# 64 rows for the last layer's pair products and the attention cells' state products, two blocks side by side in the array's row halves

## The chip, the cores and the metric

The kernel runs on one core of one Trainium2 chip. The time is device microseconds of one execution; the median of three runs is given. A profile is one further execution, recorded by the hardware profiler. The engines are called TensorE (PE, its weight loads PEld), VectorE (DVE), ScalarE (ACT), GpSimd (POOL) and SyncE (SP).

## What is computed

Four graph layers over 4096 nodes with 64 features follow each other, each as x = layernorm(x + layer(x, adj)). adj is a dense 4096 x 4096 matrix in f32.

- Layer 0 is a Chebyshev sum: three successive products with adj.
- Layer 1 has two gated cells, one over the products of the masks adj > 0 and adj < 0 with x, and one over an attention whose scores depend only on the sign of an edge. The cell's part that the change touches is the state product:

```python
gi = x @ w_ih.T + b_ih
gh = h @ w_hh.T + b_hh          # the state product
r = sigmoid(ir + hr); z = sigmoid(iz + hz); n = tanh(inn + r * hn)
return (1.0 - z) * n + z * h
```

- Layer 2 is a sum over neighbours with weights that decay with the neighbour's rank.
- Layer 3 is hyperbolic. For each pair (i, j) it needs the Moebius difference of x_i and x_j, its norm, an arctanh, and a sum over j weighted by adj. The kernel gets all pairs from one quantity per pair, a matrix product of prepared left and right sides (a "pair product"), and a second small product, here called the opposite term, that marks pairs on different sides of the unit ball.

## The kernel before

The nodes are 32 blocks of 128; four blocks are a group (8 groups), and adj is read in tiles of 512 x 512. The stages follow each other in one program for each engine. TensorE, VectorE, ScalarE and GpSimd each run their instructions in the order of the program; the order is set when the program is built, from the order of the source, and `in_order` (`tc.keep_in_program_order`) holds the marked instructions of an engine to the source's order among themselves. Waits between engines are semaphores.

1. **First pass** (to 363 us): adj is loaded, turned by TensorE (L604), copied by ScalarE (L611) and stored turned. The weights for later layers are loaded and turned meanwhile, one step a tile (`attention_weights`, `state` at L399 to L406).
2. **Second and third pass** (to 566 us). Third-pass rows end with `normed_third` (layer norm, `centre` at L298 to L302) and, some tiles later, `turned_third`, which turns the group's rows into columns of `tr_a` with `to_columns`: four transposes (L213) and one copy (L214). Row 64 of `tr_a` holds ones, for the biases. For the last row this is done by a step inside the attention stage.
3. **Attention** (to 852 us): for each group, 8 tiles of masks (VectorE L448; stored by GpSimd at L741) are multiplied with x (L1004, L1012) and adj with x (L1021). After a group, its cells are worked off one step a tile (`group_end`). `gates` (L797 to L807) does, block by block, the state product (L801: 128 rows of `tr_a`, of which 65 are used, times 260 or 256 columns) and for the edge cell the input products (L805) into the same PSUM bank. Two blocks share a PSUM tile; for the last group, whose cells run inside the decay stage, one block at a time.
4. **Decay** (to 1062 us): counts (L1242, into two column halves) give weights (L1247), which multiply x (L1198, L1210) in the array's two row halves. Groups are done in two turns of four. At a turn's end `ends` normalises the groups, `prepare` makes their left sides (`lx`, 66 columns: x, and two more) and the marks of their side of the ball (`sides`, 2 columns), and `turn_prepared` turns both with `to_columns`, eight transposes and two VectorE copies a group. The first four groups' ends fall in the second turn, the last four groups' in the pairs stage.
5. **Pairs** (from 1062 us): 36 tiles (i, j) in 72 half tiles, here called units; 64 are whole (two blocks of 128 by 512 columns), 8 on the diagonal are half as wide. For each unit `product` (L1359) multiplies two blocks of left sides with a right side (`right`, L1315 to L1319), `square` (L1368, ScalarE) and `opposite` (L1377) follow, then ScalarE Ln and Exp (L1550, L1551), VectorE L1575, ScalarE L1577 and L1586, VectorE L1560 and L1563; `turn` (L1403) transposes the factors for the mirrored tile and VectorE multiplies them in (L1405); `gather` (L1419, L1424) sums both tiles into two column halves of one bank, and VectorE adds the mirrored sums up (L1435). `less_one` is L1385. PSUM has two buffers for `product` and two for the transposes (`post`). Remaining steps (`seam`) are put in one a unit: ends of the last four groups, and each finished group's `finals`.

An f32 matmul is two instructions on TensorE, a transpose one.

Of the kernel before, what the change touches and what calls it, by code (L numbers as in the profile page):

```python
# [27 lines left out]
V_FLOOR = 2.0**-21  # L28
# [32 lines left out]
def gnn4_kernel(  # L61
# [107 lines left out]

    sp_two = keep.tile([P, NB, 2 * F], BF16, name="sp_two")  # L170
# [45 lines left out]
    def to_rows(pool, src, w):  # L216

        ps = pool.tile([P, GB, w], F32, name="post", tag="post")
        for b in range(GB):
            nc.tensor.transpose(ps[:, b, :], src[:, cols(b)], ident[0:w, 0:w])  # L220
        return ps

# [120 lines left out]
    def attention_weights(wp, wps):  # L343
# [6 lines left out]
        rows = {name: wp.tile([F + 1, H3], F32, name=f"row_{name}") for name in ("hhe", "hhn")}  # L350
        acol = wp.tile([F, 2], F32, name="acol")
# [7 lines left out]
        def load_biases(dst, name, b_ih, b_hh):  # L359
            nc.gpsimd.memset(dst, 0.0)  # L360
            nc.scalar.dma_start(dst[F : F + 1, F:GC], b_ih.unsqueeze(0))
            nc.scalar.dma_start(rows[name][F : F + 1, :], b_hh.unsqueeze(0))

        def load_rest():
# [8 lines left out]
            lambda: load_biases(whh_e, "hhe", b_ih_e, b_hh_e),  # L373
            lambda: load_biases(whh_n, "hhn", b_ih_n, b_hh_n),
# [24 lines left out]
        def state(name, dst):  # L399
            ps = turned(name)  # L400
# [5 lines left out]
            nc.vector.tensor_scalar_mul(dst[:, 0:F], dst[:, 0:F], 0.5)  # L406

# [12 lines left out]
        def score_weights():  # L420
# [17 lines left out]
            lambda: state("hhe", whh_e), lambda: state("hhn", whh_n), turned_gat, gat_and_cell, score_weights,  # L438
# [37 lines left out]
    with tc.tile_pool(name="acc", bufs=1) as acc_p, tc.tile_pool(  # L476
# [207 lines left out]
        def turned_third(g):  # L684
            to_columns(ps_p, tr_a[0 : F + 1, gcols(g)], nat_a[:, gblocks(g), :], F + 1, nc.scalar.copy)
# [47 lines left out]
    tr_o = sp_two.rearrange("p b f -> p (b f)")  # L733
# [41 lines left out]
    def group_end(g, Q, nb, tl, sums, a_t, wq, by_ln=False):  # L775
# [20 lines left out]
        def gates(ps_p, h, whh, w, pairs):  # L796
            for bs in blocks(h):  # L797
                got[bs.start] = ps = new(ps_p)
                for i in range(nb):
                    b = bs.start + i  # L800
                    in_order(nc.tensor.matmul(  # L801
                        ps[:, i, 0:w], lhsT=tr_a[:, cols(g * GB + b)], rhs=whh, start=True, stop=(not pairs)
                    ))
                    for m, (t, wt) in enumerate(pairs):
# [163 lines left out]
    def attention(signed, cols_p, sg, tl, ps_a, ps_p):  # L968
# [60 lines left out]
        else:  # L1029
# [7 lines left out]
        steps = [nothing, nothing, nothing, lambda ps_p: to_columns(  # L1037
            ps_p, tr_a[0 : F + 1, gcols(last_row)], nat_a[:, gblocks(last_row), :], F + 1, nc.scalar.copy
        )]
# [49 lines left out]
    nc.gpsimd.memset(tr_o, 0.0)  # L1089
# [3 lines left out]
    sides = const.tile([P, NB, 2], F32, name="sides")  # L1093
# [4 lines left out]
    def prepare(g):  # L1098
# [3 lines left out]
        sq = sm.tile([P, GB, F], F32, name="sq", tag="t0")  # L1102
        nc.vector.tensor_tensor(sq, xg, xg, ALU.mult)
        nc.vector.tensor_reduce(n2[:, gs], sq, AX.X, ALU.add)
        nc.vector.tensor_scalar(inside[:, gs], n2[:, gs], -1.0, 1.0, ALU.mult, ALU.add)
        nc.vector.tensor_scalar(sides[:, gs, 0], inside[:, gs], 0.0, None, ALU.is_ge)
        nc.vector.tensor_scalar(sides[:, gs, 1], inside[:, gs], 0.0, None, ALU.is_lt)
        nc.vector.tensor_tensor(side[:, gs], sides[:, gs, 0], sides[:, gs, 1], ALU.subtract)
# [3 lines left out]
        lx = sm.tile([P, GB, F + 2], F32, name="lx")  # L1112
        nc.vector.tensor_tensor(lx[:, :, F + 1], rabs[:, gs], side[:, gs], ALU.mult)
        nc.vector.tensor_tensor(lx[:, :, F], n2[:, gs], lx[:, :, F + 1], ALU.mult)
        nc.vector.tensor_tensor(lx[:, :, 0:F], xg, over_rows(lx[:, :, F + 1]), ALU.mult)
        nc.vector.tensor_tensor(nat_c[:, gs, 0 : F - 1], nat_a[:, gs, 0 : F - 1], over_rows(rabs[:, gs], F - 1), ALU.mult)
        nc.vector.scalar_tensor_tensor(nat_c[:, gs, F - 1], n2[:, gs], 1.0, rabs[:, gs], ALU.add, ALU.mult)
        left[g] = lx

    def turn_prepared(ps_p, g):  # L1120
        to_columns(ps_p, tr_a[0 : F + 2, gcols(g)], left.pop(g), F + 2, nc.vector.tensor_copy)
        to_columns(ps_p, tr_o[0:2, gcols(g)], sides[:, gblocks(g), :], 2, nc.vector.tensor_copy)

    def constants3():


        to_right = const.tile([P, F + 2], F32, name="to_right", tag="wih_pp")
        to_other = const.tile([P, 2], BF16, name="to_other", tag="wih_mm")

        spread = const.tile([P, F + 1], F32, name="spread", tag="whh_e")  # L1130
        wh_x = const.tile([P, F], F32, name="wh_x", tag="whh_n")
        nc.vector.memset(to_right, 0.0)
        nc.vector.tensor_scalar_mul(to_right[0:F, 0:F], ident[0:F, 0:F], -4.0)
        nc.vector.tensor_scalar_mul(to_right[F : F + 2, F : F + 1], ident[F : F + 2, F + 1 : F + 2], 2.0)
        nc.vector.tensor_scalar_mul(to_right[F : F + 2, F + 1 : F + 2], ident[F : F + 2, F : F + 1], 2.0)
        nc.vector.memset(to_other, 0.0)
        nc.vector.tensor_scalar_mul(to_other[0:2, 0:1], ident[0:2, 1:2], OPPOSITE)
        nc.vector.tensor_scalar_mul(to_other[0:2, 1:2], ident[0:2, 0:1], OPPOSITE)
        nc.vector.memset(wh_x, 0.0)
        nc.vector.tensor_copy(wh_x[0:F, :], wh)  # L1140
# [152 lines left out]

    with tc.tile_pool(name="o3", bufs=1) as op, tc.tile_pool(name="cols3", bufs=3) as cols_p, tc.tile_pool(
# [14 lines left out]
        for t in rvs + ros:  # L1309
            nc.gpsimd.memset(t, 0.0)  # L1310

        def right(i):
            q = seq.index(i) % 2
            ps = ps_p.tile([P, GW], F32, name="post", tag="post")
            nc.tensor.matmul(ps[0 : F + 2, :], lhsT=to_right, rhs=tr_a[:, gcols(i)], start=True, stop=True)  # L1315
            nc.scalar.copy(rvs[q][0 : F + 2, :], ps[0 : F + 2, :])
            ps = ps_p.tile([P, GW], F32, name="post", tag="post")
# [322 lines left out]
```

## Time and profile before

| | us |
|---|---|
| median of three runs | 1538.62 (1536.35 to 1538.94) |
| the profiled execution's own time | 1536.75 |
| its span, first to last instruction | 1535.0 |
| TensorE, VectorE, ScalarE, GpSimd busy in the span | 1408.3, 1064.4, 762.8, 124.4 |
| mean granted TensorE clock | 0.979 |

An engine's busy time is the union of its instructions. TensorE's instructions are pipelined and their ends are modelled, so its rate is read from the distance between starts. A row of a group reads: line, engine, operation, output <- inputs, partitions x elements and type, for a matmul the rows*columns of the array in front of it, then count, busy time, mean length, idle time before and what ended it. "Idle, by X" names the instruction whose semaphore came last. The chain of work that ended last is, by engine, 65% TensorE, 20% VectorE, 7% ScalarE and 5% DMA.

### The profile page before, as it was taken

The numbers are of one execution on the slowest core, as the hardware profiler recorded it, in microseconds if no ns is written. First come the engines' busy times: TensorE is split into PE (matmuls) and PEld (weight loads), VectorE is DVE, ScalarE is ACT, GpSimd is POOL, SyncE is SP. The second block draws the span as 40 slices with busy tenths as digits, with TensorE's granted clock in tenths as the row PEclk, the third lists the DMA queues.
The fourth block names the chain that finished last, engine by engine and source line by source line (L and its number), as shares of the span: only waits on it lengthen the run. The fifth ranks groups of instructions, "written<-read, shape, count | busy, mean of one in ns | idle before, by whom it ended". The sixth has DMA issues, their size and how long they took to land.

```text
span 1535.0 us, 19444 instructions
## 1 busy us (share of the span) xinstructions
PE 1408.3 (92%) x7054; PEld 645.1 (42%) x7054; DVE 1064.4 (69%) x2121; ACT 762.8 (50%) x1267; POOL 124.4 (8%) x194
## 2 busy tenths in 40 slices
PE   5999999999999999889999999998888999899995
PEld 3555555554444333334443333333334434344343
DVE  5889989883000675657677322645999999899997
ACT  3554444432000111212222576655877999899995
POOL 3001100000000011222222200000000000000000
PEclk9999999999999999999999999999999999999997
DMA  9999999996787998878887655453134443445330
GB/s 291 411 406 409 413 409 399 385 357 265 247 278 270 373 387 322 278 280 316 301 317 286 193 170 176 155 165 156 65 141 155 170 168 138 167 160 191 150 114 11
DMA packets 103361, 385.40 MB, mean 251 GB/s; under 512 B 16340, under 2 KB 17368, under 8 KB 71256
## 3 DMA queue, kind: packets, MB, share of 16 engines
q1 hardware_dynamic: 84256, 296.78, 54.1%
q0 software_dynamic: 15616, 85.73, 13.7%
q10 hardware_dynamic: 3384, 1.56, 0.4%
q8 instruction: 58, 0.95, 0.2%
q14 instruction: 47, 0.39, 0.1%
HBM read 297.26 MB, written 85.20 MB: 249 GB/s over the span
## 4 chain that ended last, share of the span: by engine, by line
PE 65%; DVE 20%; ACT 7%; DMA 5%; issue 3%; SPq 0%; ACTq 0%; POOL 0%; DVEq 0%; POOLq 0%
PE tp L604 7%; PE pass L512 6%; PE w_ps L512 6%; PE v_ps L1359 5%; PE sums_ps L1419 4%; PE a_ps L1021 4%; PE cnt_ps L1242 4%; PE acc_ps L1198 4%; PE pass L505 4%; PE h_ps L505 4%; DVE at_m L1405 3%; DVE rt L1575 3%; PE p_ps L1004 2%; PE post L523 2%; ACT wt L1247 2%
## 5 line engine op out<-in xcount | busy, mean ns | idle before, releaser
L611 ACT COPY at<-tp 128x512 f32<-128x512 f32 x256 | 132.5, 599 | 134.6 <-issue 93.7
L1359 PE MATMUL v_ps<-rv,tr_a 128*128 128x512 f32 (+1 forms) x288 | 138.4, 604 | 33.6 <-DVE rt L1575 29.9
L1247 ACT ACTIVATE wt<-cnt_ps 128x512 uint16<-128x512 f32 x210 | 116.4, 594 | 73.8 <-PE cnt_ps L1242 69.6
L604 PE MATMUL tp<-ident,raw 128*128 128x128 f32 x1024 | 133.2, 284 | 14.5 <-DMA raw<-in_adj_dram 9.7
L637 DVE TENSOR_REDUCE dpart<-raw 128x4 f32<-128x2048 f32 x64 | 145.4, 2272 | 0.1
L639 DVE TENSOR_REDUCE lows<-raw 128x1 f32<-128x2048 f32 x64 | 145.4, 2272 | 0.0
L1419 PE MATMUL sums_ps<-at_d,nat_c 128*64 128x512 f32 x288 | 143.2, 619 | 1.4 <-DVE at_d L1563 1.0
L604 PEld LDWEIGHTS tp<-ident,raw 128*128 128x128 f32 x1024 | 116.5, 145 | 53.5 <-issue 30.7
L1021 PE MATMUL a_ps<-at,nat_a 128*64 128x512 f32 x512 | 126.3, 622 | 2.9 <-DVE at L987 2.9
L448 DVE TENSOR_SCALAR pos<-at 128x2048 fp8e4<-128x2048 f32 x72 | 87.6, 1232 | 49.3 <-DMA at<-adj_t 43.3
L1424 PE MATMUL sums_ps<-at_m,nat_c 128*64 128x512 f32 x224 | 111.0, 618 | 0.0
L512 PE MATMUL w_ps<-at,cheb_n 128*128 128x512 f32 x224 | 101.1, 595 | 0.0
L512 PE MATMUL pass<-at,cheb_n 128*128 128x512 f32 x224 | 98.3, 596 | 0.7 <-DVE cheb_n L665 0.7
L1586 ACT ACTIVATE rt<-rt,one_col 128x1024 f32<-128x1024 f32 x72 | 78.7, 1095 | 21.6 <-DVE rt L1575 21.4
L1359 PEld LDWEIGHTS v_ps<-rv,tr_a 128*128 128x128 f32 x288 | 51.9, 195 | 82.8 <-issue 43.4
L1242 PE MATMUL cnt_ps<-m,follow 128*64 128x512 fp8e4 x480 | 81.2, 391 | 5.1 <-ACT wt L1247 2.0
L1575 DVE SCALAR_TENSOR_TENSOR rt<-v_ps,rt 128x1024 f32<-128x1024 f32 x72 | 83.4, 1159 | 3.1 <-ACT rt L1551 2.9
L1560 DVE SCALAR_TENSOR_TENSOR f<-rt,w 128x1024 f32<-128x1024 f32 x72 | 83.0, 1160 | 1.3 <-ACT rt L1586 1.3
L1563 DVE TENSOR_TENSOR at_d<-at_d,f 128x1024 f32<-128x1024 f32 x72 | 83.4, 1159 | 0.1
L1405 DVE TENSOR_TENSOR at_m<-post,at_m 128x512 f32<-128x512 f32 x112 | 75.3, 685 | 10.1 <-PE post L1403 9.5
L1368 ACT ACTIVATE w<-v_ps,one_col 128x1024 f32<-128x1024 f32 x72 | 75.7, 1053 | 11.5 <-PE v_ps L1359 11.0
L1577 ACT ACTIVATE w<-w,half_shift 128x1024 f32<-128x1024 f32 x72 | 78.6, 1094 | 0.8
(368 smaller groups left out, 2269.7 us busy)
## 6 DMA issues: line engine op xcount, KB each, us to landing
at<-adj_t SPq DMA_DIRECT2D x122, 1024.0 KB, 6.6
raw<-in_adj_dram SPq DMA_DIRECT2D x64, 1024.0 KB, 12.3
adj_t<-at POOLq DMA_DIRECT2D x64, 1024.0 KB, 8.1
at_d<-adj_t SPq DMA_DIRECT2D x36, 1024.0 KB, 4.8
at_m<-adj_t SPq DMA_DIRECT2D x28, 1024.0 KB, 6.8
mask_t<-pos POOLq DMA_DIRECT2D x64, 256.0 KB, 6.2
m<-mask_t SPq DMA_DIRECT2D x120, 128.0 KB, 2.8
m<-mask_t SPq DMA_DIRECT2D x60, 256.0 KB, 4.0
```

Source lines behind the costliest of these rows:

```text
L505: in_order(nc.tensor.matmul(ps[q * F : (q + 1) * F, :], lhsT=cheb_n[:, jb, k, :], rhs=rhs, start=first, stop=last, skip_group_check=True,))
L512: in_order(nc.tensor.matmul(ps, lhsT=cheb_n[:, jb, k : k + 2, :], rhs=rhs, start=first, stop=last))
L604: in_order(nc.tensor.transpose(tp[:, cols(b)], raw[:, b, cols(k)], ident))
L611: nc.scalar.copy(at[:, k, :], tp)
L637: in_order(nc.vector.tensor_reduce(dpart[:, g, c, :], raw, AX.X, ALU.add))
L639: in_order(nc.vector.tensor_reduce(lows[:, n : n + 1], raw.rearrange("p b j -> p (b j)"), AX.X, ALU.min))
L1021: in_order(nc.tensor.matmul(ps[q * F : (q + 1) * F, :], lhsT=nat_a[:, c * CB + k, 0:F], rhs=parts[q if signed else 0][:, k, :], start=(c = ...
L1242: in_order(nc.tensor.matmul(cnt[a][r * HP : (r + 1) * HP, :], lhsT=follow, rhs=chunks[c][odd][2 * a + r][:, k, :], start=(h == 2 * NB - 1) ...
L1247: in_order(nc.scalar.activation(wt[odd][a], cnt[a], AF.Relu, scale=-128.0))
L1359: nc.tensor.matmul(vs[n][:, k, cs], lhsT=tr_a[:, cols(jb)], rhs=rights[i][0][:, cs], start=True, stop=True)
L1419: in_order(nc.tensor.matmul(bank[0:F, :], lhsT=nat_c[:, j * CB + k, :], rhs=own[t][:, k, :], start=(i == j and k == 0), stop=(j == seq[-1] ...
L1575: nc.vector.scalar_tensor_tensor(rt, vs[n][:, :, cs], V_FLOOR, rt, ALU.max, ALU.add)
```

## The change

The left sides, the marks and the state are brought to 64 rows (features), and two neighbouring blocks are stacked: block 2m in rows 0 to 63, block 2m + 1 in rows 64 to 127. A pair product or a state product then uses 64 rows, and two neighbouring blocks use the two row halves. To make 64 rows enough, x being centred (its features sum to nothing), the 64th feature is left out: its place holds ones in the state, whose weights have the 64th column subtracted (`leave_out`) and the bias in its row, and a second quantity in the left sides. The constant 1 that was added by the bias of Square and Ln goes into the product itself.

Rows are turned by `turn_pairs` (third pass, state) and the new `turn_prepared`: two 128 x 128 transposes instead of four.

```diff
+    tr_x = tr_a[:, 0 : N // 2].rearrange("p (m n) -> p m n", n=P)
...
+    def turn_pairs(pool, g):
+        t = sm.tile([P, GB, F], F32, name="with_ones", tag="t0")
+        nc.gpsimd.memset(t[:, :, F - 1], 1.0)
+        nc.scalar.copy(t[:, :, 0 : F - 1], nat_a[:, gblocks(g), 0 : F - 1])
+        ps = pool.tile([P, GB // 2, P], F32, name="post", tag="post")
+        for m in range(GB // 2):
+            nc.tensor.transpose(ps[:, m, :], t[:, 2 * m : 2 * m + 2, :].rearrange("p b f -> p (b f)"), ident)
+        nc.scalar.copy(tr_x[:, g * GB // 2 : (g + 1) * GB // 2, :], ps)
...
+        def both_halves():
+            nc.gpsimd.memset(twice, 0.0)
+            for q in range(2):
+                nc.vector.tensor_copy(twice[0:F, q * F : (q + 1) * F], ident[0:F, 0:F])
+                nc.vector.memset(twice[F : F + 1, (q + 1) * F - 1 : (q + 1) * F], 1.0)
...
-        def state(name, dst):
-            ps = turned(name)
+        def state(name, to):
+            for t in range(2):
+                leave_out(raws[name][:, t, :])
+            ps, dst = turned(name), states[name]
...
+            w = to.shape[1]
+            ps = wps.tile([P, w], F32, name=f"state_ps_{name}", tag="post")
+            nc.tensor.matmul(ps, lhsT=twice, rhs=dst[:, 0:w], start=True, stop=True)
+            nc.scalar.copy(to, ps)
...
         def turned_third(g):
-            to_columns(ps_p, tr_a[0 : F + 1, gcols(g)], nat_a[:, gblocks(g), :], F + 1, nc.scalar.copy)
+            turn_pairs(ps_p, g)
...
+    tr_c = tr_x
+    tr_o = sp_two[:, 0 : NB // 2, :]
...
                 for i in range(nb):
                     b = bs.start + i
+                    half = slice(b % 2 * F, b % 2 * F + F)
                     in_order(nc.tensor.matmul(
-                        ps[:, i, 0:w], lhsT=tr_a[:, cols(g * GB + b)], rhs=whh, start=True, stop=(not pairs)
+                        ps[:, i, 0:w], lhsT=tr_x[half, (g * GB + b) // 2, :], rhs=whh[half, :],
+                        start=True, stop=(not pairs)
                     ))
+                for i in range(nb):
+                    b = bs.start + i
                     for m, (t, wt) in enumerate(pairs):
...
-        steps = [nothing, nothing, nothing, lambda ps_p: to_columns(
-            ps_p, tr_a[0 : F + 1, gcols(last_row)], nat_a[:, gblocks(last_row), :], F + 1, nc.scalar.copy
-        )]
+        steps = [nothing, nothing, nothing, lambda ps_p: turn_pairs(ps_p, last_row)]
...
-    nc.gpsimd.memset(tr_o, 0.0)
...
+        sides = sm.tile([P, GB, F], F32, name="sides", tag="o_sb")
+        nc.gpsimd.memset(sides, 0.0)
...
-        lx = sm.tile([P, GB, F + 2], F32, name="lx")
-        nc.vector.tensor_tensor(lx[:, :, F + 1], rabs[:, gs], side[:, gs], ALU.mult)
-        nc.vector.tensor_tensor(lx[:, :, F], n2[:, gs], lx[:, :, F + 1], ALU.mult)
-        nc.vector.tensor_tensor(lx[:, :, 0:F], xg, over_rows(lx[:, :, F + 1]), ALU.mult)
...
+        lx = sm.tile([P, GB, F], F32, name="lx")
+        nc.vector.tensor_tensor(lx, nat_c[:, gs, :], over_rows(side[:, gs]), ALU.mult)
+        left[g] = lx, sides
...
-        to_columns(ps_p, tr_a[0 : F + 2, gcols(g)], left.pop(g), F + 2, nc.vector.tensor_copy)
-        to_columns(ps_p, tr_o[0:2, gcols(g)], sides[:, gblocks(g), :], 2, nc.vector.tensor_copy)
+        ps = ps_p.tile([P, 2 * GB // 2, P], F32, name="post", tag="post")
+        ms = slice(g * GB // 2, (g + 1) * GB // 2)
+        for n, t in enumerate(left.pop(g)):
+            for m in range(GB // 2):
+                two = t[:, 2 * m : 2 * m + 2, :].rearrange("p b f -> p (b f)")
+                nc.tensor.transpose(ps[:, n * GB // 2 + m, :], two, ident)
+        nc.vector.tensor_copy(tr_c[:, ms, :], ps[:, 0 : GB // 2, :])
+        nc.vector.tensor_copy(tr_o[:, ms, :], ps[:, GB // 2 : GB, :])
...
-        for t in rvs + ros:
-            nc.gpsimd.memset(t, 0.0)
         def right(i):
...
+            for to, w, t in ((rvs[q], to_right, tr_c), (ros[q], to_other, tr_o)):
+                ps = ps_p.tile([P, GW], F32, name="post", tag="post")
+                for b in range(GB):
+                    nc.tensor.matmul(
+                        ps[:, cols(b)], lhsT=w[:, b % 2, :], rhs=t[:, (i * GB + b) // 2, :], start=True, stop=True
+                    )
+                nc.scalar.copy(to, ps)
...
-                nc.tensor.matmul(
-                    vs[n][:, k, cs], lhsT=tr_a[:, cols(jb)], rhs=rights[i][0][:, cs], start=True, stop=True
-                )
+                half = slice(jb % 2 * F, jb % 2 * F + F)
+                in_order(nc.tensor.matmul(
+                    vs[n][:, k, cs], lhsT=tr_c[half, jb // 2, :], rhs=rights[i][0][half, cs], start=True, stop=True
+                ))
...
-            nc.scalar.activation(ws[n][:, :, cs], vs[n][:, :, cs], AF.Square, bias=one_col)
+            nc.scalar.activation(ws[n][:, :, cs], vs[n][:, :, cs], AF.Square)
...
-                nc.tensor.matmul(
-                    vs[n][:, k, cs], lhsT=tr_o[:, cols(jb)], rhs=rights[i][1][:, cs], start=False, stop=True,
-                    skip_group_check=True,
-                )
+                half = slice(jb % 2 * F, jb % 2 * F + F)
+                in_order(nc.tensor.matmul(
+                    vs[n][:, k, cs], lhsT=tr_o[half, jb // 2, :], rhs=rights[i][1][half, cs],
+                    start=False, stop=True, skip_group_check=True,
+                ))
...
+            for q in range(2):
+                half = slice(q * F, (q + 1) * F)
+                nc.vector.tensor_copy(wh_x[half, q, :], spread_w[half, :])
...
-                nc.vector.scalar_tensor_tensor(rt, vs[n][:, :, cs], V_FLOOR, rt, ALU.max, ALU.add)
+                nc.vector.scalar_tensor_tensor(rt, vs[n][:, :, cs], 1.0 + V_FLOOR, rt, ALU.max, ALU.add)
...
-                nc.scalar.activation(rt, rt, AF.Ln, bias=one_col)
+                nc.scalar.activation(rt, rt, AF.Ln)
```

The constants of the last layer (`constants3`, made at the start of the decay layer's second turn) are laid out for both halves: `to_right` and `to_other` become 128 x 2 x 128, `wh_x` 128 x 2 x 64, and 22 small VectorE operations make them instead of 12. The steps of `finals` read the stacked columns with `wh_x` of the block's half, in as many matmuls as before.

## The prediction

> **What bounds the kernel now.** I read the page's 40 slices first, then the busy time by stage, then who waits for whom inside the two stages that the change touches, then the instructions of single steps. TensorE is busy for 92% of the span, but that is a mean over five stages: a first pass over the adjacency (to 363 us), two more passes (to 566), the attention layer (to 852), the decay layer (to 1062) and the last layer's pairs (to the end).
>
> By stage (columns: length, then busy time of TensorE, its weight loads, VectorE, ScalarE, GpSimd, granted clock, DMA share, GB/s):
> ```profile
> 0.00:363.00 363.00, 339.51 (x1789) 201.46 (x1790) 306.45 (x269) 155.76 (x307) 46.67 (x90) 0.99 1.01 386
> ...
> 566.00:852.00 286.00, 263.94 (x1261) 111.34 (x1260) 185.80 (x537) 59.71 (x123) 71.49 (x95) 0.97 0.82 296
> 852.00:1062.00 210.00, 201.65 (x1658) 72.73 (x1657) 82.51 (x287) 126.04 (x239) 6.23 (x10) 0.99 0.51 155
> 1062.00:1535.00 473.00, 409.63 (x1692) 183.07 (x1691) 436.08 (x827) 404.73 (x566) 0.00 (x0) 0.96 0.38 143
> ```
> The first pass is the DMA's (share 1.01). Attention and decay are TensorE's. In the pairs stage VectorE is the busiest: 436 of 473 us, TensorE 410, ScalarE 405. So a gain on TensorE there counts only where VectorE waits for it. Those waits, 1062 to 1510 us:
> ```profile
> DVE at_m L1405 <- PE post L1403: 9.5, 10, 2.2
> DVE w L1385 <- ACT w L1368: 4.8, 2, 4.0
> DVE tb L1435 <- PE sums_ps L1424: 3.6, 4, 2.4
> DVE rt L1575 <- ACT rt L1551: 2.9, 4, 1.5
> DVE tr_a L214 <- PE post L213: 1.3, 1, 1.3
> ```
> VectorE is idle for 27 of these 448 us; 15 are put down to TensorE, 10 to ScalarE. The 15 are the heart of the forecast.
>
> One pair unit on TensorE (start, length, line):
> ```profile
> 1305.49 1.98 PE L1359 MATMUL v_ps<-rv,tr_a 128*128 128x512 f32 x4 [0.36 <-DVE rt L1575]
> 1307.41 0.64 PE L1419 MATMUL sums_ps<-at_d,nat_c 128*64 128x512 f32 x1
> 1307.41 0.64 PE L1424 MATMUL sums_ps<-at_m,nat_c 128*64 128x512 f32 x1
> ...
> 1308.75 0.59 PE L1424 MATMUL sums_ps<-at_m,nat_c 128*64 128x512 f32 x1
> 1309.28 0.60 PE L1377 MATMUL v_ps<-ro,sp_two 128*128 128x512 bf16 x2
> 1309.72 0.60 PE L1403 MATMUL post<-ident,f 128*128 128x128 f32 x4
> ```
> Starts count, not lengths (ends are modelled). An f32 matmul is two instructions, 0.43 us apart. The product (two blocks, four instructions) takes 1.92 us to the next start. The sums of L1419 and L1424 go to two column halves and start together: two for the time of one. After the last of them, 1308.75 + 0.43 = 1309.18, the next form starts 0.10 us late: the price of a change of form. The opposite term takes 0.44, eight transposes 8 x 0.109 = 0.87. Unit: 1.92 + 1.87 + 0.44 + 0.87 = 5.1 us. VectorE's starts are 1.13 apart (three long operations) and 0.60 (three short): 5.2 us. ScalarE has five of about 1.0: 5.1. All three engines are level, which is why small delays become idle time.
>
> Row halves, as the change uses them, occur in the decay layer, in bf16:
> ```profile
> 959.66 0.39 PE L1198 MATMUL acc_ps<-wt,over_two 64*128 64x512 bf16 x1
> 959.66 0.39 PE L1198 MATMUL acc_ps<-wt,sup_two 64*128 64x512 bf16 x1
> 959.88 0.38 PE L1198 MATMUL acc_ps<-wt,over_two 64*128 64x512 bf16 x1
> ```
> Two start together, the next pair 0.22 later: full overlap. f32 in row halves is not in this trace. Its bounds: no overlap (1.72 us for four instructions) to full (0.86). I take full, because bf16 row halves and f32 column halves both show it.
>
> **The change, part by part.**
>
> *Pair products and opposite term.* Product 1.72 to 0.86, opposite 0.43 to 0.22: minus 1.08 us per unit. Forms now change four times per unit instead of twice: plus 0.2. TensorE's unit falls from 5.1 to 4.2. Over 64 whole and 8 half units that is some 73 - 15 us less TensorE; making the right sides in eight instructions of 128 columns and four bf16 ones instead of two and one adds 0.2 to 0.8 (at 0.11 to 0.19 each, start spacing or weight load) eight times, say 4. None of that is on the path by itself. What is: of the 15 us VectorE waits for TensorE I take 13 away. What is late next is VectorE itself, then ScalarE.
>
> *No bias in Square and the last Ln.* L1550 (Ln, no bias) is 1049 ns, L1586 (Ln, bias tile) 1142, same shapes. So 0.09 twice a unit off ScalarE, 12 us in all; on the path 2 of the 10 us that VectorE waits for it.
>
> *Preparing the sides.* Per group VectorE loses copies of 682 and 668 ns and two operations of 160, and gains two copies of 128x256 (423 for such a read of PSUM): minus 0.8. Four groups are prepared in the pairs stage, where VectorE sets the pace: minus 3.3, plus 0.4 for two 64x64 copies (180). Four transposes instead of eight save TensorE 0.44 a group; four groups fall in the decay layer, which is TensorE's: minus 1.7. There the constants take ten more small VectorE operations (about 0.15), covered by an engine busy 82 of 210 us; uncovered they cost 1.5. The last group's cells work block by block, so their eight state products overlap with nothing and only change form: plus 1. Decay layer: minus 0.5. GpSimd's dropped fills are covered already.
>
> *State products in the cells.* Around one group's edge gates:
> ```profile
> 785.96 0.71 PE L801 MATMUL post<-whh_e,tr_a 128*128 128x260 f32 x2
> 786.50 0.49 PE L805 MATMUL post<-wih_pp,p_t 128*128 128x196 f32 x2
> 786.83 0.60 PE L801 MATMUL post<-whh_e,tr_a 128*128 128x260 f32 x2
> ```
> A block's state product is two instructions, 0.22 apart. Edge: four blocks, 1.74 us, halved saves 0.87, three more changes of form cost 0.30 to 0.45. Node: 0.87 saved; one of its two pairs stands between 128x128 forms (L895, L1004), 0.2 to 0.3 more; the other already stands between L1021s. Together minus 1.1 a group. From 705 us the period is 34.6 us, TensorE busy 32.7, DMA share 0.83 to 0.91: four groups get it whole. The three before wait in part for loads; I give them half. Minus 6.
>
> *Turning rows in pairs.* The transposes now wait for a GpSimd fill and a ScalarE copy (about 0.4, as the 128x256 copy L557, 388 ns) after the centring. Two of these transposes waited for centring, 1.66 and 0.48 us: plus 1 to 3.5 if all seven do; eight times two transposes less: minus 1.7. I take 0. The last row's fill goes behind mask stores on GpSimd, which wait for VectorE (88 us in 14 waits); if it is late, TensorE stands, and everything behind the transpose with it. That can gain nothing and cost at most one load's wait, 5 us; I take 1, since TensorE waits for loads there anyway. Attention: minus 5.
>
> *Weights in the first pass.* Two small matmuls and a dozen small operations, beside a DMA queue that is full: nothing. Without that cover, 3 us.
>
> **The clock.** The granted clock falls to half for 3.41 us or its double after TensorE idles:
> ```profile
> 1309.66:1313.07 3.41, 1.32 (x10) 0.78 (x7) 3.41 (x5) 3.41 (x6) 0.00 (x0) 1.00 0.34 108
> 1313.07:1316.48 3.41, 2.80 (x4) 1.18 (x4) 3.41 (x5) 3.41 (x4) 0.00 (x0) 0.50 0.00 0
> ```
> Counting start spacings, TensorE streamed 0.27 of the first stretch. Of all such stretches, those up to 0.36 were followed by half clock, those from 0.39 not. After the change a unit streams 0.86 + 0.22 + 1.72 + 0.87 = 3.7 of 5.3 us; its emptiest 3.41 us hold about 0.22 + 0.87 + 0.43 = 1.5, or 0.45. That is close. I count eight such events in the stage instead of four. One loses 1.7 us of streaming, and a unit then has 5.2 - 4.2 = 1.0 us to spare, so about 0.9 each reaches the path: plus 3.5.
>
> Pairs stage: -13 - 2 - 2.9 + 3.5 = -14.5. Sum: 0 (passes) - 5 - 0.5 - 14.5 = **-20 us** on the profiled 1536.75 us: 1516.8. The three timed runs have a median of 1538.62, 1.9 above it: 1518.6. I say **1518**.
>
> **Two rules of the Trainium skill.** "TensorEngine Tiling (Array Packing)", Key Properties, says that changing the tiling mode drains TensorE, which speaks against a change that alternates modes; the trace prices the drain at 0.10 us against 0.86 saved. "TensorE: Matmul & The Clock Gate", Measured speedup vs the span model, has 3.07 for four row tiles, 77%. By that ratio, an estimate, the product would take 1.12 us instead of 0.86, and by the same share 4 of the 13 us would stay. That page gives three column tiles 2.38 as well, while the column halves here overlap fully, so I go by the trace.
>
> **Rivals.**
> 1. *More comes off.* All 27 us of VectorE's waits go but 6, and attention gives 8: 21 + 2.9 + 8 + 1.7 = 34, 1505; 1494 to 1509. For: in 1200 to 1250 us VectorE reaches 49.1 of 50. Against: ScalarE stays level. Chance 0.17.
> 2. *Half clock eats it.* 15 to 20 events at 0.9 take 13.5 to 18 of the 18 us gained in the pairs stage: 1529 to 1533, and 1538 if attention, still on its loads, gives none of its 5. For: 0.45 is near 0.39. Against: half clock lengthens TensorE's streams, so the clock comes back. Chance 0.17 (0.11 still faster, 0.06 level).
> 3. *No overlap, slower.* If f32 row halves run one after the other, TensorE's unit becomes 5.1 + 0.2 to 0.3 for changes of form + 0.06 for the right sides, 5.4, above VectorE's 5.2. It decides from a saving per product below 0.2 us. 64 units at 0.2 are 13, attention's five changes of 0.1 in seven groups 4; half to all of it is 1547 to 1556. Against: the two rows above. Chance 0.10.
> That nothing moves because the stage is VectorE's is rival 2's upper end. An order of the queues that comes out worse: 0.03, slower.
>
> **Numbers.** Forecast 0.53 (1509 to 1526). Faster: 0.53 + 0.17 + 0.11 = 0.81; within 0.2% (3 us, about what a measurement can tell from no change) 0.06; slower 0.10 + 0.03 = 0.13. The range, 1498 to 1538, leaves out rival 3 and the end of rival 1.
>
> **What would show it.** Right: L1359 in two simultaneous rows of 64*128, 0.43 apart, product to next start near 1.0; VectorE's wait for L1403 under 3 us; the 34.6 us period near 33.5; Square near 1.01 us. Wrong: L1359's four starts 0.43 apart one by one; a clock under 0.93 in the pairs stage; VectorE still idle for over 20 us there, or TensorE waiting on GpSimd near 566 us.

## The result and the profile after

The changed kernel takes 1521.37 us (median of four runs, 1518.61 to 1522.78) against 1538.13 (1536.35 to 1538.94): ratio 0.9897, 95% interval 0.9877 to 0.9918. The profiled execution took 1522.32 us, its span 1520.4, the mean granted clock is 0.966 (before 0.979). Lines have moved: the pair product is L1413 now, Square L1422, the opposite term L1432, the transposes of the factors L1458 and their use L1460, the sums L1474 and L1479, the mirrored sums' addition L1488 and L1490, VectorE's last step of a unit L1633, the state product L835, `turn_pairs` L230 to L234.

By stage, in the columns of the first block of the prediction:

```profile
566.00:852.00 286.00, 259.16 (x1273) 98.54 (x1270) 188.49 (x546) 62.09 (x129) 69.79 (x95) 0.98 0.83 301
852.00:1062.00 210.00, 200.28 (x1658) 71.72 (x1660) 85.33 (x309) 130.09 (x244) 3.81 (x9) 1.00 0.53 168
1062.00:1520.40 458.40, 365.50 (x1723) 156.92 (x1719) 427.86 (x796) 386.70 (x560) 0.62 (x2) 0.91 0.38 141
```

VectorE stays the busiest of the last stage, and its clock column has fallen from 0.96 to 0.91. For the accounts below the stages are cut at landmarks of the program (last transposed tile of adj, first product of the attention, first count, first pair product, end), since fixed times cut the two kernels at different work:

| stage | before, us | after, us | difference | forecast | half windows before, after |
|---|---|---|---|---|---|
| first pass | 357.7 | 357.6 | -0.1 | 0 | not counted |
| second and third pass | 211.8 | 214.9 | +3.1 | 0 | 0, 2 |
| attention | 283.2 | 276.0 | -7.2 | -5 | 5, 4 |
| decay | 209.1 | 205.6 | -3.5 | -0.5 | 1, 0 |
| pairs | 473.2 | 466.3 | -6.9 | -14.5 | 6, 19 |
| sum | 1535.0 | 1520.4 | -14.6 | -20 | 12, 25 |

A half window is 3.41 us at a granted clock of 0.50; longer stretches count as two or more; the last half-clock stretch of each program, which begins about where TensorE's work ends (17 us in the change), is left out, here and below. The last column carries the story: the total came out close to the forecast, the pairs stage gained half of what was forecast, and it ran for 64.9 us at half clock instead of 20.5.

The row halves do overlap in f32:

```profile
1240.44 1.13 PE L1413 MATMUL v_ps<-rv,tr_a 64*128 64x512 f32 x4 [0.52 <-DVE rt L1633]
1241.50 0.64 PE L1474 MATMUL sums_ps<-at_d,nat_c 128*64 128x512 f32 x1
...
1243.89 0.39 PE L1432 MATMUL v_ps<-ro,sp_two 64*128 64x512 bf16 x2 [0.45 <-ACT w L1422]
1244.21 0.66 PE L1458 MATMUL post<-ident,f 128*128 128x128 f32 x4
1245.48 0.66 PE L1458 MATMUL post<-ident,f 128*128 128x128 f32 x4 [0.61 <-DVE at_m L1460]
```

From the product's first start to the sums' first is 1.06 us; it was 1.92. The opposite term gives way after 0.32. Now read the brackets: TensorE stands 0.52, 0.45 and 0.61 us in one unit, for VectorE's last step, for Square and for the use of the transposes. It got the time, and mostly waits in it.

VectorE's waits from the first pair product on (to 1495 us), to be set against the forecast's second block:

```profile
DVE tb L1488 <- PE sums_ps L1479: 5.5, 3, 2.3
DVE at_m L1460 <- PE post L1458: 5.0, 6, 1.9
DVE rt L1633 <- ACT rt L1609: 2.8, 4, 0.9
DVE y L1221 <- PE post L1215: 2.7, 1, 2.7
DVE f L1618 <- ACT rt L1644: 2.0, 3, 0.9
```

The wait for the transposes is halved (9.5 to 5.0) and the four-microsecond wait for Square, the first of the stage, is gone; but the waits for the sums (L1488 and L1490; before, L1433 and L1435) have grown from 4.0 to 6.7, and the stage now opens with a wait for L1215.

### The profile page after: what moved, and what is told of

Its sections match the earlier page's. It is cut to its first block, busy times and chain, and to the rows that moved or that the text cites. A ratio compares the mean times of both kernels' runs of the same rounds, so it can differ in the third digit from the quotient of the medians.

```text
span 1520.4 us, 19563 instructions
## 1 busy us (share of the span) xinstructions
PE 1358.4 (89%) x7082; PEld 605.2 (40%) x7082; DVE 1060.8 (70%) x2129; ACT 752.3 (49%) x1277; POOL 122.4 (8%) x206
## 3 DMA queue, kind: packets, MB, share of 16 engines
q0 software_dynamic: 15616, 85.73, 13.8%
## 4 chain that ended last, share of the span: by engine, by line
PE 53%; DVE 27%; ACT 9%; DMA 6%; issue 4%; ACTq 0%; SPq 0%; POOL 0%; DVEq 0%; POOLq 0%
PE pass L541 7%; PE tp L633 6%; PE w_ps L541 6%; PE a_ps L1058 4%; PE cnt_ps L1295 4%; PE acc_ps L1251 4%; PE pass L534 4%; DVE at_m L1460 4%; DMA raw<-in_adj_dram 3%; DVE rt L1633 3%; DVE f L1618 3%; PE h_ps L534 3%; DVE at_d L1621 3%; PE p_ps L1041 2%; PE sums_ps L1474 2%
## 5 line engine op out<-in xcount | busy, mean ns | idle before, releaser
L1474 PE MATMUL sums_ps<-at_d,nat_c 128*64 128x512 f32 x288 | 153.6, 659 | 2.2 <-DVE at_d L1621 1.0
L1479 PE MATMUL sums_ps<-at_m,nat_c 128*64 128x512 f32 x224 | 119.3, 659 | 0.0
L1413 PE MATMUL v_ps<-rv,tr_a 64*128 64x512 f32 (+1 forms) x288 | 85.6, 674 | 33.9 <-DVE rt L1633 33.8
L1644 ACT ACTIVATE rt<-rt 128x1024 f32<-128x1024 f32 x72 | 72.2, 1006 | 26.9 <-DVE rt L1633 26.6
L1633 DVE SCALAR_TENSOR_TENSOR rt<-v_ps,rt 128x1024 f32<-128x1024 f32 x72 | 83.1, 1155 | 2.9 <-ACT rt L1609 2.8
L1458 PE MATMUL post<-ident,f 128*128 128x128 f32 x448 | 70.4, 286 | 14.9 <-DVE at_m L1460 13.3
L1609 ACT ACTIVATE rt<-w,half_shift 128x1024 f32<-128x1024 f32 x72 | 79.2, 1100 | 0.7
L1460 DVE TENSOR_TENSOR at_m<-post,at_m 128x512 f32<-128x512 f32 x112 | 75.3, 682 | 5.5 <-PE post L1458 5.0
```

Source lines behind the costliest of these rows:

```text
L1460: work.append(lambda to=to, tp=tp: nc.vector.tensor_tensor(to, tp, to, ALU.mult))
L1474: in_order(nc.tensor.matmul(bank[0:F, :], lhsT=nat_c[:, j * CB + k, :], rhs=own[t][:, k, :], start=(i == j and k == 0), stop=(j == seq[-1] ...
L1633: nc.vector.scalar_tensor_tensor(rt, vs[n][:, :, cs], 1.0 + V_FLOOR, rt, ALU.max, ALU.add)
```

## Experiments

**Theory.** TensorE's freed time turns into standing time; a 3.41 us window in which TensorE does too little is followed by half clock, and TensorE is then late for VectorE. **Rivals**: the missing gain lies in shared buffers that make TensorE stand (`turn_pairs`), in the order of the queues, or in one half of the change that cost more than thought.

**e1_cells and e2_pairs: each half of the change alone.** e1 keeps the state products and their turning (`turn_pairs`) and has the pairs stage of before; e2 has the reverse.

> Only the cells' half of the change (state products in row halves, rows turned in pairs); the last layer as before. In the profile of the change attention took 7.2 us less and the passes before it 2.9 us more, so by my account 4 to 5 us remain: 1533 to 1535 against 1538 for before, with the pairs stage at 473 us and its clock at 0.96 as before. The rival, that the last layer is VectorE's and nearly all of the 17 us come from the cells, expects 1524 or less.

> Only the last layer's half of the change; cells as before. By my account the pairs stage gives 7 and the decay layer 2 to 3.5: 1527 to 1530, the third pass without its 3 us stall, a clock near 0.91 to 0.93 in the pairs stage. The rival that the cells carry the gain expects 1535 or more. If the two halves add up, the savings of the two runs sum to about 17 us.

Measured: e1 1528.52 us, ratio 0.9942 (0.9917 to 0.9967); e2 1530.9, 0.9959 (0.9938 to 0.998). The product of the ratios is 0.990, as for the change: within intervals of a quarter per cent to either side the halves add up. (The medians alone, against 1534.82 us for the kernel before in the same session, give 6.3 and 3.9 us, less than the 17 expected together.) Each profile is of the longest of its kernel's runs (1532.14 and 1535.58 us). The pairs stage takes 473.4 us in e1 and 467.0 in e2, with 8 and 21 half windows: they come with the pairs' part. The passes take 216.2 us in e1 and 211.8 in e2: their loss comes with the cells' part, `turn_pairs`; how much of it, the table below shows.

**e3_own: another buffer for the rows to be turned.**

```diff
-        t = sm.tile([P, GB, F], F32, name="with_ones", tag="t0")
+        t = sm.tile([P, GB, F], F32, name="with_ones", tag="o_sb")
```

> The change, with the turned rows' tile (with_ones) in a buffer that the split of the next rows does not use. If the shared buffer costs TensorE the stand of 3 us and the half clock after it near 550 us, attention starts 3 us earlier and the time is 1518 to 1519. The rival, that the loads of attention hide it, expects 1521 to 1522, with attention's first product earlier and its last one not.

Measured: 1523.9 us, ratio 0.9915 (0.9891 to 0.9938), no better than the change itself. What it was aimed at, on TensorE in the changed kernel:

```profile
548.75 0.44 PE L233 MATMUL post<-ident,with_ones 128*128 128x128 f32 x2
552.36 0.41 PE L233 MATMUL post<-ident,with_ones 128*128 128x128 f32 x2 [3.17 <-ACT with_ones L230]
```

TensorE stands 3.17 us for ScalarE's copy, which itself waits for the last step of VectorE's split of the rows (L244); the split's temporary tile has the same buffer. Before, at this place:

```profile
550.86 0.62 PE L213 MATMUL post<-ident,nat_a 128*65 128x128 f32 x4 [0.48 <-DVE nat_a L302]
```

In e3_own the 3.17 us are 1.21, and the half window at 553 us is gone; but its passes take 215.4 us, because two half windows fell at 366.8 and 373.7, among waits of TensorE that before has too (0.78, 0.46, 0.86 and 0.72 us) and that brought it none.

That came clear only from all profiles together. In all fourteen, the length of the two passes goes by the number of half windows in them:

| half windows | us | profiles |
|---|---|---|
| 0 | 211.8 | before, e2_pairs |
| 1 | 213.0 to 213.3 | f1, f2, f3, g1, g2, g4 |
| 2 | 214.8 to 215.4 | the change, e3, e4 |
| 3 | 216.2 to 216.6 | e1, f0, g0 |

So about 1.6 us for each (1.3 to 1.9 from row to row), and next to nothing else: the 3.17 us stand costs its half window, no more. Half windows lie on a fixed grid of 3.413 us, and whether the waits near 370 us fill one of its windows differs between kernels that are alike up to there. It differs between executions of one kernel too: 49 runs of the kernel before had spans of 1527.7 to 1542.5 us with 52 to 89 us at half clock, and the two go together (correlation 0.64).

The pairs stage of e3_own gives a second price, since its three compute engines go through the same instructions in the same order as the change's. Its units take the change's time within 0.12 us, all but two. The two are among four units in a row in which the change had half clock and e3_own none. These four, in the change and then in e3_own:

```profile
1079.66:1103.69 24.03, 19.08 (x71) 7.40 (x70) 20.46 (x41) 20.61 (x21) 0.62 (x2) 0.79 0.25 89
```

```profile
1081.17:1101.65 20.48, 15.14 (x71) 6.29 (x70) 20.09 (x40) 19.07 (x20) 0.62 (x2) 1.00 0.29 104
```

Three half windows, 3.5 us: VectorE's work is nearly the same (20.46 and 20.09), it is idle for 3.6 us in the one and 0.4 in the other. In the first four units it is e3_own that has more half clock (15.1 us for 10.2), and they take the same time: a half window costs only where TensorE is waited for. The other 16 half windows of the change have no such partner, so their price is not shown one by one.

**e4_fill: products with zero weights, to keep TensorE going.** Three pairs a unit, 0.65 us, added into the product's bank behind the opposite term, ahead of the next product:

```diff
+            for _ in range(3):
+                for k in range(HB):
+                    half = slice(k * F, k * F + F)
+                    in_order(nc.tensor.matmul(
+                        vs[n][:, k, cs], lhsT=zw[half, :], rhs=rights[i][1][half, cs],
+                        start=False, stop=True, skip_group_check=True,
+                    ))
```

> The change, plus three pairs of products with zero weights a unit (0.65 us of TensorE, added to the values of the unit, so nothing changes) in the gap ahead of the next product. It adds work and takes none away. Theory: half clock after idle stretches took the gain of the pairs stage; then the clock there comes back to 0.97 or more, half-clock stretches fall from 14 to 6 or fewer, VectorE's 15 us of waits for TensorE fall under 7, and the time is 1512 to 1517. Rival: VectorE and ScalarE are the limit and the clock is a symptom; then the clock comes back and the time stays at 1520 to 1523.

Measured: 1550.97 us, ratio 1.0096 (1.0071 to 1.012), pairs stage 493.9, 16 half windows. Inconclusive: the new instructions made the build order all three queues anew (Square behind the last Ln, the opposite term behind the transposes), and VectorE now waits 17.8 us for ScalarE's Exp and 9.1 for Square. A probe has to hold the order fixed.

**f0 to f3: the same with the order fixed.** In f0_fixed every instruction of the pairs stage on VectorE, ScalarE and TensorE keeps the order of the source. f1_fill adds the three zero pairs, f2_bias a zero bias tile in Square and the last Ln, f3_twice does each pair product twice. VectorE and ScalarE go through the same lists in f0, f1 and f3.

```diff
-            for k in range(HB):
+            for k in (0, 1, 0, 1):
```

> The change, with every TensorE, VectorE and ScalarE instruction of the pairs stage held to the order of the source (transposes before the opposite term, so that they no longer stand behind its wait for Square). It is the base for the next three kernels, which change one thing under the same order. If the order of the queues costs VectorE part of its waits, 1512 to 1518; if half clock does, about 1521 as the change, with some 14 half-clock stretches again; an order that suits the engines worse, 1525 to 1550.

> The fixed order, plus three pairs of products with zero weights a unit behind the opposite term (0.65 us of TensorE a unit, the values stay the same). Theory: half clock is what holds the stage up; then half-clock stretches fall to a third or less and the stage is 5 to 12 us shorter than in the fixed order, although TensorE does 45 us more. Rival: VectorE and ScalarE set the pace; then the stage is as long as in the fixed order within 2 us, or longer by what the added work is in the way.

> The fixed order, with a tile of zeros as the bias of Square and of the last Ln, so that ScalarE has the 0.09 us twice a unit again. If ScalarE's relief counts, 2 to 6 us slower than the fixed order; if ScalarE has cover, within 2 us.

> The fixed order, with each pair product done twice (the second overwrites the first): TensorE has the 0.86 us a unit back that the row halves took off, and nothing else changes. If the halved product is what the pairs stage gained by, 8 to 20 us slower than the fixed order; if half clock gave that back, half-clock stretches fall to 6 or fewer and the time is within 4 us of the fixed order.

| | us | ratio, 95% interval | half clock in the pairs stage, us | VectorE's waits for TensorE, us |
|---|---|---|---|---|
| f0_fixed | 1670.85 | 1.0868 (1.0829 to 1.0908) | 198.0 | 80.9 |
| f1_fill | 1636.59 | 1.0672 (1.0643 to 1.0701) | 99.0 | 50.3 |
| f2_bias | 1671.38 | 1.0889 (1.086 to 1.0919) | 180.9 | 75.1 |
| f3_twice | 1709.22 | 1.1129 (1.1099 to 1.1158) | 126.3 | 110.9 |

The whole stage in f0_fixed and in f1_fill:

```profile
1055.30:1669.10 613.80, 419.34 (x1751) 186.91 (x1749) 466.28 (x823) 395.85 (x566) 0.62 (x2) 0.82 0.29 111
```

```profile
1053.30:1634.60 581.30, 421.39 (x2177) 187.60 (x2177) 466.30 (x823) 395.50 (x566) 0.62 (x2) 0.90 0.31 117
```

426 more matmul records, nearly the same busy time of TensorE, the same work of VectorE and ScalarE, clock 0.90 for 0.82, and the stage is 32 us shorter. Work that does nothing made the kernel faster; an explanation by the order of the queues is excluded, since the order is the same. One unit of both, the same 8 and 6 instructions of VectorE and ScalarE:

```profile
1478.04:1485.87 7.83, 5.99 (x22) 2.05 (x22) 5.90 (x8) 4.61 (x6) 0.00 (x0) 0.78 0.57 239
```

```profile
1451.29:1457.48 6.19, 4.82 (x28) 1.98 (x28) 5.90 (x8) 4.52 (x6) 0.00 (x0) 1.00 0.73 302
```

One half window, 1.64 us. Of 17 units that have one in f0 and none in f1, 15 differ by 1.53 to 1.66. f2_bias answers another question: with a bias tile Square takes 1.095 instead of 1.004 us and the last Ln 1.136 instead of 1.044, as the forecast had it, but here ScalarE is not on the path and no time is lost. f3_twice, expected 8 to 20 us or at most 4 us above f0_fixed, is 38 above it: the 0.86 us a unit, 58 us in all, stand on the path, and 72 us less of half clock would give back about the rest, at the price above; that last part is an estimate.

f0 itself is 150 us slower than the change, far above everything expected of it, which the theory doesn't explain. So a fixed order nearer to the change's own was tried.

**g0, g1, g2, g4: the unit's order written out.** g0_order has each unit as the change's trace has most of them (Square ahead of Exp, the opposite term ahead of the transposes). g2_fill2 and g1_fill3 add two and three zero pairs between the transposes and the next product; main instructions keep one order in all three.

> The changed kernel with the order of each unit's main instructions written out as the trace of the changed kernel has it in most units (Ln, Square, Exp, Exp, Ln on ScalarE; product, sums, opposite, transposes on TensorE; the two products with the mirrored tile on either side of the one with the own tile on VectorE); only small steps between units are left to the build. It is the base for the two runs beside it. Both theories: 1513 to 1530 us, pairs stage 460 to 475 us, half clock 10 to 20 stretches there (the changed kernel: 466 us, 14 stretches of 65 us in all).

> g0_order and, in each unit, two pairs of 64-row products with zero weights, 0.43 us of TensorE, between the transposes and the next product, where TensorE stands about 0.5 us for VectorE. They add zero and nothing new waits for them. Theory (the half clock took the missing gain; price 0.34 us for each us of it, from units 4 to 7 of the changed kernel against e3_own, and 0.35 from f1_fill against f0_fixed): half clock in the pairs stage falls from some 60 to under 20 us, VectorE's waits for TensorE from about 14 to 5 to 9 us, the time to 10 to 20 us under g0_order, about 1505. Rival (the waits come of the queues' order, the clock only shows them): within 3 us of g0_order.

> g0_order and three pairs of zero-weight products in the same place, 0.65 us of TensorE a unit. Theory (half clock): the same fall of half clock as with two pairs; where the 0.65 us pass the 0.5 us that TensorE stands, up to 0.15 us a unit of TensorE are added, most of which VectorE does not wait for: within 5 us of g2_fill2, 5 to 20 us under g0_order. Rival (order of the queues): 0 to 10 us above g0_order, since work is added and nothing taken off.

Measured: g0 1721.61 us, ratio 1.1217 (1.1181 to 1.1254); g2 1684.74, 1.096 (1.0916 to 1.1003); g1 1674.8, 1.0902 (1.0871 to 1.0932); half clock in the pairs stage 283.3, 153.6 and 119.5 us. The level missed the forecast by 200 us, the difference bore the theory out again, at more than it was taken for: 37 and 47 us faster with more work (g1, expected within 5 us of g2, is 10 faster). Where the 200 us come from, in g0_order (VectorE's wait, then TensorE's):

```profile
DVE at_m L1460 <- PE post L1458: 161.5, 52, 5.2
```

```profile
PE v_ps L1413 <- DVE rt L1635: 160.2, 59, 4.2
```

A ring: VectorE's use of the transposes waits for them, they stand behind the sums and the next product, and that waits for VectorE's last step (the buffer). In the change's trace VectorE uses the transposes of the unit before, so there is no ring. g4_lagged puts that lag, and two zero pairs, into the written order:

```diff
-                gathers[n + 1] = (t, h, before)
+                gathers[n + 2] = (t, h, before)
```

> g2_fill2 with the products with the mirrored tile (VectorE) one unit later than the transposes that they read, as the trace of the changed kernel has them, and the sums one unit later for it; in g0_order they were in the unit of their transposes, which closed a ring in each unit (VectorE's last product, pair product, sums, opposite term, transposes, VectorE again: 0.96 + 1.76 + 0.28 + 0.94 + 0.6 + 1.13 + 0.6 + 1.13 = 7.4 us, where g1_fill3 has 7.1 to 7.9). Without the ring a unit is VectorE's own work, 5.2 to 5.6 us. Theory (ring for the slowness of g0_order to g1_fill3, half clock for the gain that the changed kernel lacks): half clock in the pairs stage under 20 us (changed kernel 65), VectorE's waits for TensorE 3 to 8 us (14), pairs stage 448 to 460 us (466), time 1500 to 1515 us. Rival (order of the queues at the seams, not the clock): half clock falls as well, the waits stay at 12 us or more, 1515 to 1535 us. If the ring is not the reason for g0_order, over 1600 us.

Measured: 1585.69 us, ratio 1.036 (1.0333 to 1.0387), above the theory's 1500 to 1515 and the rival's 1535, below the 1600 that would have spoken against the ring; pairs stage 526.8. The ring was the reason: the wait of at_m is gone, and units 25 to 32 take 44.7 us against 44.8 in the change; no other eight in a row come that close. What is left against the change: VectorE waits 24.3 us for ScalarE's Exp and 13.8 for the diagonal tiles' transposes, at the places where other steps stand between units, and half clock stays at 95.6 us. So no version here beats the change, and whether filling pays in the change's own order remains open: each attempt changed the order too.

## Why the prediction was nearly right in sum and wrong in its largest part

**By its own signs.** Of the signs that the prediction named for being right, the product to the next start (1.06 us), Square (1.009) and the period of attention (33.7) came; the wait for the transposes came out at 5.0 us, not under 3. Of its signs for being wrong, two came as well, a clock under 0.93 in the pairs stage and over 20 us in which VectorE is idle:

```profile
1054.10:1495.00 440.90, 360.58 (x1682) 152.51 (x1682) 417.26 (x739) 381.63 (x515) 0.62 (x2) 0.93 0.41 153
```

64.9 us at half clock make the 0.93 here 0.926 (0.91 to the end of the program), and VectorE is idle for 23.6 us; it was 27.

**Overlap, price of a change of form.** Right: product 1.92 to 1.06 us to the next start, which is 0.86 less, with the 0.10 for a change of form twice in it. Rival 3 fell at once. The Trainium skill's "TensorE: Matmul & The Clock Gate", Measured speedup vs the span model, weighed in the prediction, would have given an estimate of 1.12 + 0.20 = 1.32 us; the measurement decides for full overlap of two row halves.

**Less work on VectorE and ScalarE.** The work itself, right to the decimal: VectorE's busy time in the pairs stage went from 436.08 to 433.19 us, -2.9. The bias:

```profile
L1644 ACT ACTIVATE rt<-rt 128x1024 f32<-128x1024 f32 x64 | 67.2, 1054 | 20.6 <-DVE rt L1633 20.3
L1422 ACT ACTIVATE w<-v_ps 128x1024 f32<-128x1024 f32 x64 | 64.6, 1009 | 7.7 <-PE v_ps L1413 7.5
```

1142 and 1101 ns before. VectorE's waits for ScalarE over 0.15 us fell from 9.6 to 6.1, where -2 was forecast. But 3.2 of these 3.5 us are one wait, the first of the stage, for the first Square (VectorE stood 3.97 us until 1065.00; 3.2 of them lie in the stage). In the change the stage opens with VectorE's 2.74 us for L1215, 2.0 of them in the stage. Without the two openings the waits for ScalarE went from 6.4 to 6.1: of the 2 us for the bias, next to nothing reached the path.

**"Of the 15 us VectorE waits for TensorE I take 13 away", and half clock +3.5.** This is the step that failed. The waits sum to 14.9 us before and 14.4 after. Parted by whether a half window lies in them or ended less than 2 us ahead:

| VectorE's waits for TensorE, pairs stage, us (times) | before | change | e2_pairs | e3_own | e1_cells |
|---|---|---|---|---|---|
| away from half clock | 10.7 (15) | 4.5 (4) | 4.5 (4) | 4.0 (3) | 11.4 (15) |
| at half clock | 4.2 (2) | 9.9 (9) | 10.2 (9) | 7.3 (6) | 3.7 (3) |

The change did to the ordinary waits what it was to do, if less: -6.2. Half clock put +5.7 back. Sum of the stage: -2.9 - 3.5 - 6.2 + 5.7 = -6.9, as measured. With the openings by themselves (3.2 us for ScalarE before, 2.0 for TensorE in the change): -2.9 for the work, -1.2 for the opening, -0.3 for ScalarE, -8.2 for the ordinary waits in the units (10.7 to 2.5), +5.7 for half clock. Two terms were mis-sized. Of the 15 us, 4.2 were half clock's already and 2.5 of the rest stay: 8 and not 13 were to be had. And the events: fourteen, of 19 windows, not the eight that were counted. The count came from one regular unit, 0.45 of a window streamed at its emptiest. In the pairs stages of six profiles (both kernels, f0, f1, g0, g1), of the windows at full clock that streamed under 0.37 of their time 141 of 148 were followed by half clock, of those between 0.37 and 0.41 11 of 32, of the 552 above none (512 columns counted as 0.427 us in f32, half of it in narrower types): the threshold was right. But a window in which TensorE stands for VectorE is emptier than the forecast's unit, and nine of the fourteen stretches lie in the first 160 us of the stage, where the last groups' ends stand between units. What the clock took shows in how the two kernels run against each other there (from the first pair product to VectorE's last step of a unit):

| unit | before: us, half clock so far | change: us, half clock so far | change ahead by |
|---|---|---|---|
| 24 | 159.2, 13.7 | 161.8, 47.8 | -2.6 |
| 48 | 303.5, 20.5 | 299.4, 54.6 | 4.1 |
| 66 | 414.1, 20.5 | 405.5, 64.9 | 8.6 |

In the first third the change lost with 34 us more half clock; from there on it gained 11.2 us with 10 more. Rival 2 named this mechanism, at 13.5 to 18 us; it took about 6 more than before.

**Attention, -5.** Measured -7.2, with one half window less; at the 1.6 us that a window costs in the passes, -5.6. The gates show the halving:

```profile
716.19 0.71 PE L835 MATMUL post<-whh_e,tr_a 64*128 64x260 f32 x4
716.83 0.93 PE L842 MATMUL post<-wih_pp,p_t 128*128 128x196 f32 x4
```

Two blocks in 0.64 us to the next form; one took 0.54. The period from 705 us on is 33.7 us (34.6 before, 33.5 forecast). The stage varies, though: 270.7 to 276.0 us in the twelve profiles with this part (two to four half windows), 283.2 and 288.0 in the two without it (five and six). The means lie 12 us apart, so the 7.2 of this pair of profiles is rather low, and the forecast lower still; why there are fewer half windows with the change is open.

**Turning rows, taken at 0.** Wrong in kind: TensorE waits at 552 us for ScalarE, whose copy waits for the buffer of VectorE's split, a wait that the prediction did not have; the price is a half window. One of the passes' two windows is this; the other lies among waits that before has as well.

**Decay, -0.5.** -3.5 came: one half window (3.4 us long) that before has and the change has not, some 1.6 of it, and about -2 for the rest. All profiles bear that out: with the pairs' part the stage takes 205.6 us with no half window, 208.1 to 209.1 with two and 209.5 to 210.5 with three; without it 209.1 with one and 211.8 with three, so about 2 us more at the same number. They fit the 1.7 of the transposes, without the 1 that the last group's cells were to cost; no run takes the two apart.

So that the total lay near the forecast was luck in part: +3 in the passes and +8 in the pairs stage stood against -5 in attention and decay.

## What to carry to other kernels

Before counting a saving on an engine, ask which of the waits that it is to shorten are at full clock, and what the engine does with the freed time: if it stands, price the half clock in every stretch of the stage, the irregular ones above all, not in one typical unit. Half windows are to be counted by stage in each profile before two kernels are compared: here they go with whole differences of 1.6 to 5 us that look like effects of code. A probe that adds or takes instructions must hold the queues' order, or its time tells of the order.

## What was not expected of the hardware

- Half clock needs no long idle stretch. The window ahead of the half clock at 1269.77 us, on TensorE:

```profile
1266.15 0.66 PE L1451 MATMUL post<-ident,f 128*128 128x128 f32 x4
1266.64 1.00 PE L1533 MATMUL post<-spread,tb 128*128 128x65 f32 x8
1269.21 1.57 PE L1413 MATMUL v_ps<-rv,tr_a 64*128 64x512 f32 x4 [1.57 <-DVE rt L1633]
```

  The longest wait is 1.57 us; the window streamed 0.34 of its time. The Trainium skill, "TensorE: Matmul & The Clock Gate", Why this matters for your kernels, advises "No PE-idle gaps >~3µs between matmul bursts"; by that rule no half clock would have followed here. What decided in these runs is the share streamed in a window of a fixed 3.413 us grid, about 0.4.
- Products with zero weights count as work for the clock: 0.43 to 0.65 us of them a unit took 34 to 47 us off kernels whose TensorE stood on the path.
- A half window costs 1.6 us where TensorE sets the pace (passes, f0) and 1.2 where it partly does (3.5 us for three, above): 0.34 to 0.48 us for each of its microseconds. g2 and g1 against g0 give 0.28 and 0.29, their added work included.
